# Two attention layers on one core: where a phase issues side products, divisors, loads and normalizations

## The chip, the cores and the metric

The kernel runs on one core of a Trainium2 chip. The metric is the device time of one execution in microseconds; the median of several executions is compared. A core has five engines with a queue each: TensorE (PE, its weight loads shown as PEld), VectorE (DVE), ScalarE (ACT), GpSimd (POOL) and SyncE (SP). Here SP issues most of the DMAs, POOL a few small ones.

## What is computed

Two layers on x of shape (4, 256, 64, 64), all in float32; each is a group norm (32 groups), an attention and a residual:

```python
# layer A (0): 4096 queries against 1024 keys, 8 heads of 32
q = einsum('oc,bchw->bohw', Wq, x)                 # x here is _gn(x)
k = conv2x2_stride2(x, Wk);  v = conv2x2_stride2(x, Wv)
attn = softmax((q.k + q.(rel_h + rel_w)) * 32**-0.5)
x = x_in + attn.v
# layer B (1): 4 areas of 1024 tokens, 8 heads of 32
qkv = conv1x1(x, w_qkv) + b_qkv                    # x here is _gn(x)
out = softmax(q.k * 32**-0.5).v                    # within an area
out = out + depthwise_conv7x7(v_full, w_pe) + b_pe
x = x_in + conv1x1(out, w_proj) + b_proj
```

## The kernel before, in words

**Units, steps, phases.** A block is one layer of one batch element: A0 to A3, then B0 to B3. A block has 16 units: 8 chunks of 512 queries, twice 4 heads each; 128 units in all. A unit has 8 steps, one for each 128 keys. A step is four score products (keys on the partitions, 512 queries each), exp on ACT, the product of p with v accumulated in one PSUM bank `av`, and an addition of p into `acc` on DVE, from which the softmax's divisors come. A *phase* works on one and a half steps: three PSUM pairs of scores, so three exponentials of 128x1024 (two at line 334, `exp_full`, the third, of two half steps, at line 345, `exp_half`). There are 683 phases.

**A phase in the order of issue** (the main loop at the end of `direct_path`): `scores(f)` issues the score products (line 296) on PE. Then the exponentials `exps[0]`, `exps[1]`, `exps[2]` on ACT. Between them stand `add_ready`, which issues the additions of the phase before (line 369, DVE), and, where a unit ends within the phase, the last weighted products of the old unit (`accumulate`, line 359) and `evict`, the copy of `av` to SBUF as `av_sb` (line 961, ACT, two buffers). Then come the planned actions (`do`), the divisors or side parts, the weighted products of the phase before, perhaps more side parts, and another `evict`. The scheduling is manual: every engine gets its instructions in the order in which the code issues them, apart from a merge of the engines' streams.

**The score banks.** The three pairs change roles from phase to phase: the first half product of the next phase needs the pair that the second exponential has read, the first full product that of the first, the second full product that of the third.

**Side work.** All other products on PE go as *tasks* through the deque `side` and one PSUM bank (`ps_side`, tag `side`, one buffer): k0ps, v0ps, q0ps (layer A's k, v, q), k1ps, q1ps, vals_ps (layer B's k, q, v), conv_ps (the depthwise convolution as matrix products) and ops (the projection). A task is a generator of 2 or 4 *parts*; `advance` runs one. Its last part also issues the copy out of the bank, on ACT, or for ops an addition into `xm` on DVE (line 682). `need` runs tasks early where a consumer is already due. `task` appends; `soon_tasks` puts tasks behind the first one.

**The plan.** `at(g, j, f)` puts an action at step j of unit g; `do` runs all actions of the steps that a phase covers: loads (SP's DMAs), normalizations on ACT (`normalize`, line 261, in place on hq, hv, h, or into taps), additions, statistics, and the tasks' entry into `side`. `plan_norm` makes the group statistics: `aggregate` (DVE, line 230), `means` (a product gm on PE, line 235, a copy and three small DVE operations), two steps later `variances` (a product gv, line 243, and three POOL operations).

**Divisors.** When all of a unit's additions have been issued, the unit is in `to_divide`. `divisors` sums acc over the partitions by products with ones (line 378, into the side bank `den`), and `divide` copies it to `den_sb` (line 395, ACT) and sends four rows by DRAM into `few` (lines 396 and 397, POOL). At step (g+2, 0) `reciprocals` (lines 403 to 407) inverts `few` on DVE and broadcasts it by DRAM into `rb` (one buffer). At (g+2, 4) `multiply` (line 410, DVE) makes `att` from `av_sb` and `rb`. Behind it come layer A's `add_residual` and `store_chunk` (lines 534 to 540), or layer B's `add_conv` (line 667) and `project`.

Of the kernel before, what the change touches and what calls it, by code (L numbers as in the profile page):

```python
# [24 lines left out]
NKT = MK // P  # L25
# [34 lines left out]
def direct_path(  # L60
# [125 lines left out]

    side = deque()
    now, last = [-1], len(BLOCKS) * UNITS * NKT  # L190

    def task(parts, f, *args):
        side.append([parts, f(*args)])

    def soon_tasks(tasks):

        for n, (parts, f, *args) in enumerate(tasks):
            side.insert(1 + n, [parts, f(*args)])

    def advance():  # L200
        side[0][0] -= 1
        next(side[0][1], None)
        if side[0][0] == 0:
            side.popleft()

    def need(made, key):
        while key not in made:
            advance()
        return made[key]


    stats, norms = {}, {}

# [5 lines left out]
    def plan_norm(key, g, j):  # L219

        name = f"{key[0]}{key[1]}"
        made = {}

        def aggregate():
            for tag, cols in (("mv", 2), ("gmean", 1), ("dev", 1), ("gvar", 1)):
                shape = [P, CT, cols] if cols > 1 else [P, CT]
                made[tag] = pool.tile(shape, FP, tag=tag, name=f"{tag}_{name}", bufs=2)
            mv = made["mv"]
            for t in range(CT):
                V.bn_aggr(out=mv[:, t, :], in_=stats[key][:, t].rearrange("p c s -> p (c s)"))  # L230

        def means():
            mv, mean, dev = made["mv"], made["gmean"], made["dev"]
            ps = ps_side(f"gm_{name}")[:, :CT]
            T.matmul(ps, lhsT=gmat, rhs=mv[:, :, 0], start=True, stop=True)
            S.copy(mean, ps)
            V.tensor_sub(dev, mv[:, :, 0], mean)
            V.tensor_mul(dev, dev, dev)
            V.tensor_add(dev, dev, mv[:, :, 1])

        def variances():
            ps = ps_side(f"gv_{name}")[:, :CT]
            T.matmul(ps, lhsT=gmat, rhs=made["dev"], start=True, stop=True)
            S.activation(made["gvar"], ps, AF.Identity, bias=eps)
            norm = pool.tile([P, 2, CT], FP, tag="norm", name=f"norm_{name}", bufs=8)
            shift, rstd = norm[:, 0, :], norm[:, 1, :]
            G.tensor_tensor(rstd, made["gvar"], neghalf, ALU.pow)
            G.tensor_tensor(shift, made["gmean"], rstd, ALU.mult)
            G.tensor_scalar(shift, shift, -1.0, None, ALU.mult)
            norms[key] = shift, rstd  # L250

        at(g, j, aggregate)
        at(g, j + 1, means)
        at(g, j + 3, variances)

    def normalize(key, dst, src, t, by_vector=False):
        shift, rstd = norms[key]
        if by_vector:
            V.tensor_scalar(dst, src, rstd[:, t : t + 1], shift[:, t : t + 1], ALU.mult, ALU.add)
            return  # L260
        S.activation(dst, src, AF.Identity, bias=shift[:, t : t + 1], scale=rstd[:, t : t + 1])  # L261
# [121 lines left out]
    def divide(g, unit):  # L383

        if g == len(units) - 1:

            rb = pool.tile([P, CH], FP, tag="p", name="rb", bufs=PB)
            V.reciprocal(rb, dens[g])  # L388
            V.tensor_mul(unit[4]()[:, unit[0], :], avs.pop(g), rb)  # L389
            spare.extend((dens.pop(g), rb))  # L390
            return
        den_sb = pool.tile([P, CH], FP, tag="den", name="den_sb", bufs=1)
        few = pool.tile([P, 2, CH // HD], FP, tag="few", name="few", bufs=2)
        rows = dram.tile([4, CH], FP, tag="rows", name=f"rows_{g}", bufs=4)
        S.copy(den_sb, dens.pop(g))  # L395
        G.dma_start(rows, den_sb[0:P:HD, :])  # L396
        G.dma_start(few[:, 0, :], rows.rearrange("h (q n) -> (h q) n", n=CH // HD))  # L397
        made = {}

        def reciprocals():  # L400
            rb = made["rb"] = pool.tile([P, CH], FP, tag="rb", name="rb", bufs=1)
            recs = dram.tile([4, CH], FP, tag="recs", name=f"recs_{g}", bufs=4)
            V.reciprocal(few[:, 1, :], few[:, 0, :])
            V.tensor_reduce(sums[:, :, g], few, AX.X, ALU.add)  # L404
            G.dma_start(recs.rearrange("h (q n) -> (h q) n", n=CH // HD), few[:, 1, :])  # L405
            for h in range(4):
                G.dma_start(rb[HD * h : HD * h + HD, :], recs[h : h + 1, :].to_broadcast([HD, CH]))  # L407

        def multiply():
            V.tensor_mul(unit[4]()[:, unit[0], :], avs.pop(g), made["rb"])  # L410

        at(*((g + 2, 0) if g < len(units) - 2 else (g + 1, 6)), reciprocals)
        at(g + 2, 4 if g < len(units) - 2 else 0, multiply)

    def att_of(key):
        if key not in atts:
# [4 lines left out]
    def plan_a(b, u, prep):  # L421
# [108 lines left out]
        def load_residual(c):  # L530
            xcs[c] = load_chunk(b, c, "xc")
# [10 lines left out]
        for c in range(NCH):  # L542
            g = u + 2 * c
            at(g - 3, 4, lambda c=c: fetch(c))
            for t in range(CT):
                at(g - 2, 1 + 2 * t, lambda c=c, t=t: norm_chunk(c, t))
            for qd in range(2):
                at(g - 2, 4, lambda c=c, qd=qd: task(2, make_q, c, qd))
            at(g + 2, 4, lambda c=c: load_residual(c))
            at(g + 3, 5, lambda c=c: add_residual(c))  # L550
            at(g + 3, 6, lambda c=c: store_chunk(c))
        return [
            (
                n % 2,
# [9 lines left out]
    def plan_b(b, u):  # L564
# [148 lines left out]
                    V.tensor_scalar(bad, count, -1.0, float(P), ALU.mult, ALU.add)  # L713

        for c in range(NCH):
            g, j = u + 2 * c + 3, 5
            if b == B - 1 and c == NCH - 1:
                for t in range(CT):
                    at(g - 2, 2 + t, lambda c=c, t=t: load_rest(c, t))
                at(g - 2, 4, lambda c=c: load_residual(c))  # L720
                at(g - 1, 1, lambda c=c: add_conv(c, [0]))
                at(g - 1, 3, lambda c=c: project_last(c))
                continue
            for t in range(CT):
                at(g - 1, 3 + 4 * t, lambda c=c, t=t: load_rest(c, t))
            at(g, 2, lambda c=c: load_residual(c))
            at(g, j, lambda c=c: add_conv(c))
            at(g, j + 2, lambda c=c: soon_tasks([(2, project, c, to) for to in range(CT)]))
        return [
# [186 lines left out]
    for i, (layer, b) in enumerate(BLOCKS):  # L916
        u = i * UNITS
        if layer == "A":
            units += plan_a(b, u, u - UNITS)
            plan_norm(("B", b), u + UNITS + 1, 7)  # L920
        else:
            units += plan_b(b, u)
    plan_zeros(2)
    for b in range(B):
        for c in range(NCH):
            plan_values(b, c, (17.8, 42, 54.5, 67)[b] + (2.0, 1.5, 1.3, 2.2)[b] * c)
        for n in range(C // 16):
            plan_conv(b, n, (36, 58, 75.5, 93.5)[b] + (1.36, 1.06, 1.1, 1.1)[b] * n)

# [47 lines left out]
    def side_parts(budget):  # L977

        mine, done = side[0] if side else None, 0
        while done < budget and side and side[0] is mine:  # L980
            advance()
            done += 1

    f = step = 0
    before = []
    while f < PHASES or before or plan or side or to_add or to_divide:
        now[0] = step
        exps = scores(f) if f < PHASES else [lambda: None] * 3
        exps[0]()
        due = bool(to_divide)  # L990
        add_ready()
        due = bool(to_divide) if f >= PHASES else due
        cut = next((n for n in range(1, len(before)) if before[n][0] // NKT != before[0][0] // NKT), 0)
        for s, u in before[:cut]:
            accumulate(s, u)
        exps[1]()
        if cut:
            evict(before[0][0] // NKT)
        exps[2]()
        while step < -(-3 * (f + 1) // 2):  # L1000
            do(*divmod(step, NKT))
            step += 1
        waiting = sum(n for n, _ in side)
        whole = side[0][0] if side else 0
        if due:
            g = to_divide.popleft()
            divisors(g, *([last - 1] if g == final else []))
            if g < final:
                divide(g, units[g])
        else:  # L1010
            side_parts(2)
        for s, u in before[cut:]:
            accumulate(s, u)
        add_ready()
        if due:
            side_parts(4)
        elif whole > 2 or waiting > 7:
            side_parts(2)
        if before:
            evict(before[-1][0] // NKT)  # L1020
        before = []
        if f < PHASES:
            full, half = parts_of(f)
# [600 lines left out]
```

## Time and profile before

| what | us |
|---|---|
| median of 3 runs (3458.95 to 3462.72) | 3460.3 |
| the profiled execution, device time | 3467.67 |
| its span | 3465.9 |
| PE busy with matmuls / with weight loads | 3186.5 / 1394.4 |
| DVE busy (of it additions, line 369) | 2526.4 (2123.7) |
| ACT busy (of it exponentials, lines 334 and 345) | 2468.6 (2036.5) |
| POOL busy | 486.1 |
| granted TensorE clock, mean | 0.977 |

ACT's 2036.5 is 1162.2 + 619.6 into p and 167.2 + 87.5 into acc. Busy time is the union of an engine's instructions; matmuls overlap each other and their ends are modelled. A row of waits gives the engine and line that waited, the engine and line whose end released it, and the total, the number and the longest of these waits. A mean over the span hides that phases differ: they hold no side part, or up to five.

### The profile page before, as it was taken

How to read it: one execution, taken by the hardware profiler on the slowest of the kernel's cores; microseconds unless marked ns; L12 is line 12 of the kernel's file. 1: busy time of each engine (PE TensorE's matmuls, PEld its weight loads, DVE VectorE, ACT ScalarE, POOL GpSimd, SP SyncE). 2: the span in 40 equal slices, each digit the busy share in tenths (PEclk: the TensorE clock that was granted, in tenths of full speed). 3: DMA queues.
4: the chain of work that ended last, by engine and by line, in shares of the span. 5: the costliest groups of instructions: out<-in, count | busy, mean ns of one | idle time of the engine just before them, and what ended most of it. 6: DMA issues, size and time to landing. Idle time of an engine off the chain costs nothing. (4 is left out here: it accounts for less than half of the span.)

```text
span 3465.9 us, 87567 instructions
## 1 busy us (share of the span) xinstructions
PE 3186.5 (92%) x36218; PEld 1394.4 (40%) x36218; DVE 2526.4 (73%) x2719; ACT 2468.6 (71%) x2988; POOL 486.1 (14%) x923
## 2 busy tenths in 40 slices
PE   7999898999989998888999999999999999999997
PEld 4444333443334443333434344444334444433332
DVE  3677786667867767676677677777678777788887
ACT  3777676776767777676777677777667777777775
POOL 0111111111111111111111111111111111111111
PEclk9999999999999999999999999999999999999998
DMA  4232333354544456556766675765555555422222
GB/s 169 54 82 72 82 95 78 85 114 99 124 98 119 127 128 157 126 133 145 182 174 168 146 174 137 180 177 146 142 131 138 147 151 141 130 63 77 77 51 54
DMA packets 648233, 422.26 MB, mean 122 GB/s; under 512 B 411772, under 2 KB 556636, under 8 KB 647832
## 3 DMA queue, kind: packets, MB, share of 16 engines
q1 hardware_dynamic: 619384, 380.11, 43.2%
q0 software_dynamic: 28448, 36.48, 4.5%
q8 instruction: 292, 4.78, 0.6%
q14 instruction: 109, 0.89, 0.1%
HBM read 318.32 MB, written 98.09 MB: 120 GB/s over the span
## 5 line engine op out<-in xcount | busy, mean ns | idle before, releaser
L369 DVE TENSOR_TENSOR acc<-acc,p 128x1024 f32<-128x1024 f32 x1790 | 2123.7, 1220 | 716.7 <-PE av L359 322.5
L334 ACT ACTIVATE p<-s 128x1024 f32<-128x1024 f32 x1194 | 1162.2, 1026 | 479.8 <-PE s L296 445.0
L345 ACT ACTIVATE p<-s 128x1024 f32<-128x1024 f32 x598 | 619.6, 1036 | 8.2 <-DVE acc L369 4.3
L296 PE MATMUL s<-q,k_A 32*128 32x256 f32 (+1 forms) x5464 | 591.7, 520 | 22.4 <-ACT p L334 17.9
L296 PE MATMUL s<-q,k_B 32*128 32x256 f32 (+1 forms) x5456 | 569.8, 513 | 12.5 <-ACT p L334 11.7
L359 PE MATMUL av<-p,v_A 128*32 128x256 f32 (+1 forms) x4784 | 473.6, 503 | 0.0
L296 PEld LDWEIGHTS s<-q,k_A 32*128 32x128 f32 x5464 | 327.3, 186 | 332.8 <-issue 89.1
L296 PEld LDWEIGHTS s<-q,k_B 32*128 32x128 f32 x5456 | 332.8, 184 | 312.6 <-issue 87.5
L359 PE MATMUL av<-p,v_B 128*32 128x512 f32 (+1 forms) x4776 | 453.6, 490 | 0.0
L407 POOL DMA_DIRECT2D rb<-recs x508 | 252.0, 501 | 448.7 <-DMA recs<-few 373.5
L405 POOL DMA_DIRECT2D recs<-few x127 | 69.7, 549 | 1571.4 <-DVE sums L404 1302.4
L359 PEld LDWEIGHTS av<-p,v_A 128*32 128x32 f32 x4784 | 146.7, 112 | 264.4 <-issue 234.6
L359 PEld LDWEIGHTS av<-p,v_B 128*32 128x32 f32 x4776 | 145.3, 110 | 262.2 <-issue 236.8
L334 ACT ACTIVATE acc<-s 128x1024 f32<-128x1024 f32 x172 | 167.2, 1025 | 109.3 <-PE s L296 109.3
L378 PE MATMUL den<-acc,ones 128*32 128x512 f32 x1024 | 150.0, 627 | 25.9 <-DVE acc L369 12.9
L164 PE MATMUL ops<-cv,wp_sb 128*32 128x512 f32 x1024 | 132.9, 637 | 37.3 <-DVE cv L667 25.6
L164 PE MATMUL q0ps<-hq,wq_sb 128*32 128x512 f32 x1024 | 127.8, 611 | 31.4 <-ACT hq L261 22.2
L164 PE MATMUL vals_ps<-hv,wqkv_sb 128*32 128x512 f32 x1024 | 127.1, 611 | 30.6 <-ACT hv L261 19.0
L164 PE MATMUL k1ps<-h,wqkv_sb 128*32 128x512 f32 x1024 | 122.8, 597 | 10.3 <-ACT den_sb L395 10.3
L397 POOL DMA_DIRECT2D few<-rows x127 | 71.2, 561 | 434.1 <-DMA rows<-den_sb 426.0
L164 PE MATMUL k0ps<-taps,wkv 128*32 128x256 f32 x2048 | 125.9, 394 | 5.8 <-ACT den_sb L395 2.8
L396 POOL DMA_DIRECT2D rows<-den_sb x127 | 74.6, 588 | 385.3 <-ACT den_sb L395 382.2
(99 smaller groups left out, 2179.5 us busy)
## 6 DMA issues: line engine op xcount, KB each, us to landing
rows<-vals SPq DMA_DIRECT2D x384, 195.9 KB
rb<-recs POOLq DMA_DIRECT2D x508, 64.0 KB, 3.2
share<-vals SPq DMA_DIRECT2D x128, 195.9 KB
vala<-vout SPq DMA_DIRECT2D x128, 144.0 KB
vals<-vout SPq DMA_DIRECT2D x128, 144.0 KB
vc<-vala SPq DMA_DIRECT2D x64, 288.0 KB
band<-mats SPq DMA_DIRECT2D x96, 176.0 KB
hq<-in_x SPq DMA_DIRECT2D x32, 512.0 KB
```

Source lines behind the costliest of these rows:

```text
L164: T.matmul(out[cols, :], lhsT=lhsT[:, cols], rhs=rhs, start=start, stop=stop)
L296: return T.matmul(out, lhsT=unit[2]()[rows, unit[0], j * P : (j + 1) * P], rhs=unit[1]()[rows, cols], start=True, stop=True)
L334: S.activation(p, (a, b)[n], AF.Exp, scale=SCALE)
L345: S.activation(p, c.rearrange("p b (l n) -> p b l n", l=2), AF.Exp, scale=SCALE)
L359: T.matmul(out, lhsT=v[:, j, unit[0] * P + HD * h : unit[0] * P + HD * h + HD], rhs=rhs, start=(j == 0 and not u), stop=(j == NKT - 1), sk ...
L369: V.tensor_add(to, to, p)
L378: T.matmul(dens[g][HD * h : HD * h + HD, :], lhsT=ones, rhs=p(h), start=(n == 0), stop=(n == len(sets) - 1),)
L396: G.dma_start(rows, den_sb[0:P:HD, :])
L397: G.dma_start(few[:, 0, :], rows.rearrange("h (q n) -> (h q) n", n=CH // HD))
L405: G.dma_start(recs.rearrange("h (q n) -> (h q) n", n=CH // HD), few[:, 1, :])
L407: G.dma_start(rb[HD * h : HD * h + HD, :], recs[h : h + 1, :].to_broadcast([HD, CH]))
```

## The change

It touches the order of issue alone; no product, addition or byte is added or left out.

1. A task in `side` carries a mark, set when its first part has run; `begun()` tells whether the first task is under way.
2. In a phase the second exponential is issued ahead of an ending unit's weighted products, and the third after the divisors or side parts. The actions (`do`) go to the phase's end.
3. Side parts: two per phase (one if no more than three parts wait); two more after the weighted products only where fewer than two were run, over five wait and no task is under way (always at the end, when no phase is left). Before: two, and up to four more.
4. Divisors wait until no task is under way.
5. `means` and `variances` go through a deque `quick`, one at a phase's end when no task is under way; `normalize` runs them early where it needs them.
6. `multiply` goes from (g+2, 4) to (g+3, 0). Behind it residual loads, `add_residual`, `store_chunk`, `add_conv`, its loads and the projections go four steps later too; the statistics of layer B as well, and the values of the first batch element 0.6 units.

```diff
 def task(parts, f, *args):
-        side.append([parts, f(*args)])
+        side.append([parts, f(*args), False])
...
     def advance():
         side[0][0] -= 1
+        side[0][2] = True
         next(side[0][1], None)
...
+    def begun():
+        return bool(side) and side[0][2]
+
+    def soon(f):
+
+        if now[0] < 0:
+            f()
+        else:
+            quick.append(f)
...
-        at(g, j + 1, means)
-        at(g, j + 3, variances)
+        at(g, j + 1, lambda: soon(means))
+        at(g, j + 3, lambda: soon(variances))
...
-        at(g + 2, 4 if g < len(units) - 2 else 0, multiply)
+        at(*((g + 3, 0) if g < len(units) - 3 else (g + 2, 6) if g < len(units) - 2 else (g + 2, 0)), multiply)
...
-            at(g + 2, 4, lambda c=c: load_residual(c))
-            at(g + 3, 5, lambda c=c: add_residual(c))
-            at(g + 3, 6, lambda c=c: store_chunk(c))
+            at(g + 3, 0, lambda c=c: load_residual(c))
+            at(g + 4, 1, lambda c=c: add_residual(c))
+            at(g + 4, 2, lambda c=c: store_chunk(c))
...
-            g, j = u + 2 * c + 3, 5
+            g, j = (u + 2 * c + 4, 1) if b < B - 1 or c < NCH - 2 else (u + 2 * c + 3, 7)
...
-                at(g - 1, 3 + 4 * t, lambda c=c, t=t: load_rest(c, t))
-            at(g, 2, lambda c=c: load_residual(c))
+                at(g - 2, 7 + 4 * t, lambda c=c, t=t: load_rest(c, t))
+            at(g - 1, 6, lambda c=c: load_residual(c))
...
-            plan_norm(("B", b), u + UNITS + 1, 7)
+            plan_norm(("B", b), u + UNITS + 2, 3)
...
         exps[0]()
-        due = bool(to_divide)
         add_ready()
         due = bool(to_divide) if f >= PHASES else due
+        exps[1]()
         cut = next((n for n in range(1, len(before)) if before[n][0] // NKT != before[0][0] // NKT), 0)
         for s, u in before[:cut]:
             accumulate(s, u)
-        exps[1]()
         if cut:
             evict(before[0][0] // NKT)
-        exps[2]()
-        while step < -(-3 * (f + 1) // 2):
-            do(*divmod(step, NKT))
-            step += 1
-        waiting = sum(n for n, _ in side)
-        whole = side[0][0] if side else 0
-        if due:
+        waiting = sum(n for n, *_ in side)
+        used = 0
+        if due and not begun():
+            used = 1
             g = to_divide.popleft()
             divisors(g, *([last - 1] if g == final else []))
             if g < final:
                 divide(g, units[g])
         else:
-            side_parts(2)
+            used = side_parts(2 if waiting > 3 or due else 1)
+        exps[2]()
         for s, u in before[cut:]:
             accumulate(s, u)
         add_ready()
-        if due:
-            side_parts(4)
-        elif whole > 2 or waiting > 7:
+        if not begun() and used < 2 and waiting > 5 or f >= PHASES:
             side_parts(2)
         if before:
             evict(before[-1][0] // NKT)
+        if quick and not begun():
+            quick.popleft()()
+        while step < -(-3 * (f + 1) // 2):
+            do(*divmod(step, NKT))
+            step += 1
```

More of the change, by code (lines that the diff above doesn't have):

```diff
@@ L185, in at @@
         plan.setdefault((g, j), []).append(f)
-    side = deque()
+    side, quick = deque(), deque()
     now, last = [-1], len(BLOCKS) * UNITS * NKT
     def task(parts, f, *args):
-        side.append([parts, f(*args)])
+        side.append([parts, f(*args), False])
     def soon_tasks(tasks):
         for n, (parts, f, *args) in enumerate(tasks):
-            side.insert(1 + n, [parts, f(*args)])
+            side.insert((1 if side and side[0][2] else 0) + n, [parts, f(*args), False])
     def advance():
         side[0][0] -= 1
+        side[0][2] = True
         next(side[0][1], None)
@@ L252, in plan_norm @@
         at(g, j, aggregate)
-        at(g, j + 1, means)
-        at(g, j + 3, variances)
+        at(g, j + 1, lambda: soon(means))
+        at(g, j + 3, lambda: soon(variances))
     def normalize(key, dst, src, t, by_vector=False):
+        while key not in norms:
+            while begun():
+                advance()
+            quick.popleft()()
         shift, rstd = norms[key]
@@ L925, in direct_path @@
         for c in range(NCH):
-            plan_values(b, c, (17.8, 42, 54.5, 67)[b] + (2.0, 1.5, 1.3, 2.2)[b] * c)
+            plan_values(b, c, (18.4, 42, 54.5, 67)[b] + (2.0, 1.5, 1.3, 2.2)[b] * c)
         for n in range(C // 16):
@@ L982, in side_parts @@
             done += 1
+        return done
     f = step = 0
     before = []
-    while f < PHASES or before or plan or side or to_add or to_divide:
+    while f < PHASES or before or plan or side or quick or to_add or to_divide:
         now[0] = step
         exps = scores(f) if f < PHASES else [lambda: None] * 3
+        due = bool(to_divide)
         exps[0]()
-        due = bool(to_divide)
         add_ready()
         due = bool(to_divide) if f >= PHASES else due
+        exps[1]()
         cut = next((n for n in range(1, len(before)) if before[n][0] // NKT != before[0][0] // NKT), 0)
@@ L1020, in direct_path @@
             evict(before[-1][0] // NKT)
+        if quick and not begun():
+            quick.popleft()()
+        while step < -(-3 * (f + 1) // 2):
+            do(*divmod(step, NKT))
+            step += 1
         before = []
```

## The prediction

> **What bounds the kernel now.** I read the busy shares first, then who PE waits for, then who DVE waits for, then single phases on the time line, with the windows' granted clock beside them.
>
> ```profile
> PE 3186.5 (92%) x36218; PEld 1394.4 (40%) x36218; DVE 2526.4 (73%) x2719; ACT 2468.6 (71%) x2988; POOL 486.1 (14%) x923
> ```
>
> PE is the bound, but a busy PE here isn't a PE at its peak. So I cut the trace at the first score weight load (L296) of each phase. From 82.94 to 3432.42 us there are 682 phases, 3349 us. Typical ones, as windows (us from:to, length, busy time of PE, PEld, DVE, ACT, POOL, clock, DMA):
>
> ```profile
> 2426.50:2429.68 3.18, 3.01 (x36) 1.44 (x32) 3.15 (x4) 1.99 (x3) 0.00 (x0) 1.00 0.76 202
> 1833.69:1838.35 4.66, 4.66 (x52) 1.96 (x48) 4.59 (x7) 3.43 (x4) 0.55 (x1) 1.00 0.61 169
> 1843.01:1849.44 6.43, 5.73 (x60) 2.12 (x56) 3.29 (x3) 3.78 (x5) 2.31 (x5) 1.00 1.04 154
> 2441.84:2456.79 14.95, 7.95 (x48) 2.06 (x48) 11.15 (x11) 5.06 (x5) 0.56 (x1) 0.66 0.43 121
> ```
>
> The first has no side part, the second two, the third divisors and two parts, the fourth two parts and a stall. Undisturbed phases with one part are 3.80 long, with two 4.66, with four 6.40: a part is 0.853 and a phase without any would be 2.95. It is 3.18, because the first half product needs the bank of the second exponential: too little work for PE, so ACT sets its length. Nominal length of all: 682 x 2.95 + 1075 parts x 0.853 = 2932; so some 415 us are lost. PE's waits tell where (us, times, longest):
>
> ```profile
> PE av L359 <- ACT av_sb L961: 47.5, 42, 1.5
> PE ops L164 <- DVE cv L667: 25.6, 8, 7.0
> PE q0ps L164 <- ACT hq L261: 22.2, 10, 2.3
> PE vals_ps L164 <- ACT hv L261: 19.0, 5, 6.3
> PE conv_ps L890 <- ACT den_sb L395: 12.1, 14, 2.1
> PE gm_B L235 <- DVE mv_B L230: 11.2, 3, 4.7
> ```
>
> and behind the long ones stands DVE, which waits for the broadcast reciprocals in front of `multiply`:
>
> ```profile
> DVE att_A L410 <- DMA rb<-recs: 70.7, 21, 9.6
> DVE att_B L410 <- DMA rb<-recs: 32.2, 10, 7.0
> ```
>
> The fourth window shows the whole chain on the time line (start, duration, engine, line; in brackets the idle time before it and what ended it):
>
> ```profile
> 2445.50 0.69 DVE L410 TENSOR_TENSOR att_B<-av_sb,rb 128x512 f32<-128x512 f32 x1 [7.03 <-DMA rb<-recs]
> 2446.11 3.68 DVE L369 TENSOR_TENSOR acc<-acc,p 128x1024 f32<-128x1024 f32 x3
> 2447.42 2.16 ACT L334 ACTIVATE p<-s 128x1024 f32<-128x1024 f32 x2 [3.59 <-DVE acc L369]
> 2449.71 2.10 DVE L667 SCALAR_TENSOR_TENSOR cv<-cv,bpe_sb,att_B 128x512 f32<-128x512 f32 x2
> 2450.89 3.64 PE L164 MATMUL ops<-cv,wp_sb 128*32 128x512 f32 x16 [7.00 <-DVE cv L667]
> ```
>
> DVE stands 7.03 us at `multiply`; the additions come late, so the exponentials find no free p; `add_conv` comes late, so PE stands 7.00 at the projection, and then runs at half clock (0.66 in the window). This phase loses 14.95 - 4.66 = 10.3 us. 29 phases lose over 3 us each, 164 in all; in 39 phases the granted clock is under 1, always in whole stretches of 3.4, 6.8 or 10.2 us at one half, begun in or just after such a stall. The clock is thus no cause of its own: it goes with the stalls.
>
> [...]
>
> So the 415 us are: 156 phases without side part and eviction at 0.81 (0.22 of their own, and 0.59 in the next one, whose second full score product waits for the late third exponential) = 126; waits for av_sb 47.5; waits of the seven side products for den_sb, 45.8 by the same list; the rest, 196, are stalls with their half clock.
>
> **The change, part by part.** Work on PE, ACT, DVE and the bytes moved stay what they are; all is order. The counts are from the order of the instructions in the two built programs.
>
> *Even side parts.* Phases with 0, 1, 2, 3, 4, 5 parts (divisors count one): before 198, 77, 296, 42, 60, 8; after 49, 233, 355, 44, 0, 0, with 1075 parts in both. Without side part and eviction there are 37 instead of 156: 37 x 0.81 = 30 (before 126). Evictions with too little work behind them to cover av_sb: 38 instead of 42 waits, shorter ones, since in 26 of them a part stands between (before in none): 31 (before 47.5). Phases with four or five parts, where PE waits for the copy of one task before the next (6.40 and more), are gone.
>
> *The third exponential after the side parts.* On ACT, the copies of side products stood behind L345; now 87 + 40 den_sb and 333 others stand ahead of it. For den_sb with two parts behind (third window; den_sb at 3.92 to 4.52 in its phase, the next product at 4.57 instead of 3.65) the copy now starts at 3.01 and PE needn't wait: 45.8 goes to nearly 0. The price: the third exponential ends later. In an undisturbed phase it starts 3.01 and ends 4.04 after the phase's start; with a 0.60 copy ahead it ends at 4.55 (that is where it ends today in phases with av_sb ahead of it); behind a two-part product, which is ready 2.0 us after its first weight load at 1.52 (k1ps: 1847.59, its copy 1849.58), at 5.05 to 5.15. The next phase's second full product takes it without loss until 0.27 after that phase's start, and is late by all that comes after (in the trace its weight load follows the exponential's end by 0.05). With lengths 3.80 and 4.66: one part and den_sb, 4.55 - 3.80 - 0.27 = 0.44 to 0.48, x 87 = 38; one part with another copy 0.45 x 70 = 32; two parts 0.12 x 220 = 27; two parts, copy and av_sb 0.79 x 39 = 31; three parts nothing. Sum 128. Bounds: 0, if the score products' other half covers it, and 230, if every copy ahead costs 0.5; I take 128, by the rows with av_sb ahead.
>
> [...]
>
> *Multiplications later* (from 4 steps after the reciprocals to 8; by phases 2 to 4 before, 4 to 6 after, so some 22 us instead of 9 to 17). Waits so far reached 9.6 us beyond that: the 102.9 us of DVE waits go. What is late next: `few` for the reciprocals (2 phases after the divisors in 10 units instead of 3; only 5.2 us of waits today), cheap. The residual loads, `add_residual`, `store_chunk`, `add_conv`, the conv loads and the projections move by the same 4 steps with the same distances; on SP's queue they now stand behind the side stores of their phase. Side products come 2 to 3.5 phases later in the mean; the tightest, a q of layer B, is still done 2 phases ahead of its scores (7 before), k 7 (13), the last convolution 22 (25). None is forced early by a consumer.
>
> *Loads, normalizations, statistics at the phase's end.* A task can no longer start in the phase that issues its normalization: 22.2 + 19.0 of waits go with their half clock, and with `soon` the gm_B and gvar waits (11.2 and 6.9). ACT has the normalizations (0.83 to 1.25 us) behind a later third exponential: some 200 phases, of which those with the 1.25 form delay the next first exponential by about 0.4; I take 20, bounds 0 and 50.
>
> *What is left of the 196.* The first two phases lose 12 and little changes there; den waits for acc (12.9) depend on DVE's lag, which gets less. I take 45; bounds 10 and 196.
>
> *End.* The projections of the next to last chunk move into the tail, in front of the last reciprocal (3.35): one product and xm, about +3.
>
> **Sum:** 30 + 31 + 128 + 20 + 45 = 254 lost instead of 415: -161, +3 for the end: -158. The profiled execution took 3467.7 (span 3465.9), 7 over the median of the timed runs, 3460.3. Against that median: 3460 - 158 = 3302.
>
> **Rivals.**
> 1. *Stalls only move* (d stays). For it: it's not shown that every long stall comes from rb; some normalizations wait on late exponentials alone. Against: in the three longest an rb wait of 4.6 to 7.0 us stands just ahead. With 140 to 196 left instead of 45, the gain is 63 down to 7: 3397 to 3453.
> 2. *Slower: eviction waits for `multiply`.* av_sb has two buffers, so the eviction of unit g waits for the multiplication of g-2. It stood 3 to 4 phases and 8 to 10 additions ahead; now 1 phase and 0 to 2 additions. While ACT waits, the third exponential and the next unit's first products do too. The additions (paired with the exponentials in order) end 4.2 us after them in the median, 7.7 or more in the worst tenth, and the multiplication has about a phase and a half, some 6 us. Against it: the lag falls at a unit's end, where three exponentials have no addition. It decides from 158 / 127 = 1.25 us a unit; with 2 us: +254, 3302 + 254 = 3556.
> 3. *Copies cost nothing*, stalls all gone: 30 + 31 + 10 + 10 lost, -330: 3130; half their price, 3195.
>
> **How the numbers follow.** Forecast 0.62 (3235 to 3390: the bounds of its terms, 0 to 50 and 10 to 120, about the taken ones); rival 1 0.18 (3390 to 3455, 0.02 of it no change); rival 2 0.10 (a tenth of it no change); rival 3 0.10 (3130 to 3235, a fifth of it over 3220). The range 3220 to 3450 leaves out rival 2, most of rival 3 and the end of rival 1, 2 in 10. Within 0.2% (7 us, what a measurement can tell from no change) 0.03, slower 0.09, faster 0.88.
>
> **What would show it.** Right: DVE's waits for rb under 10 us, hq, hv and cv gone from PE's list, a mean granted clock over 0.99 (0.977 now), phases of two parts at 4.7 to 4.9, one-part phases with den_sb at 4.2 to 4.3. New on PE's list would be s <- ACT p L360 with 100 or more. Wrong: av_sb waiting for DVE att on ACT's list (rival 2), or ops, vals_ps and q0ps still with gaps over 3 us (rival 1).

## The result, and the profile after

The changed kernel takes 3250.2 us (median of four, 3247.9 to 3252.4) against 3461.5 us for the kernel before on the same chip: ratio 0.938, 95% interval 0.936 to 0.941. It is 211 us faster; 158 were forecast. The profiled execution took 3248.9 us (span 3246.8).

The busy times first (engine, busy us, share of the span, instructions):

```profile
PE 3130.2 (96%) x36218; PEld 1357.5 (42%) x36218; DVE 2526.9 (78%) x2719; ACT 2485.4 (77%) x2988; POOL 489.6 (15%) x923
```

Instructions and work are the same; PE's own busy time fell by 56 us, which goes with fewer stretches at half clock (mean granted clock 0.995 instead of 0.977). Who PE waits for now (us, times, longest):

```profile
PE av L374 <- ACT av_sb L976: 30.8, 44, 2.3
PE s L311 <- ACT p L360: 21.9, 17, 10.6
...
PE s L311 <- ACT p L349: 10.7, 22, 1.3
PE ops L164 <- DVE cv L682: 4.4, 1, 4.4
...
PE k0ps L164 <- ACT den_sb L410: 2.9, 1, 2.9
```

(The lines stand 15 further down in the code: L349 is the full exponential, L360 the third, L384 the addition, L410 the copy to den_sb, L425 `multiply`.) The normalized inputs hq and hv are gone, cv is left once, in the tail, den_sb for the seven side products nearly gone. DVE's list, of which three lines answer to the question asked before:

```profile
DVE vout L824 <- DMA vals<-vout: 20.0, 2, 12.9
DVE few L418 <- DMA few<-rows: 19.8, 7, 5.2
...
DVE att_B L425 <- DMA rb<-recs: 0.5, 1, 0.5
```

The 102.9 us for rb are 0.5. A new wait stands at the head: two of 20.0 us in all for the store of vals to leave a buffer.

Cut into phases as before, the 682 phases take 3131.1 us instead of 3349.5. Against 2.96 us a phase and 0.853 a part, 198.3 us are lost instead of 416.7. By the phases' number of side parts, with those that lose over 3 us each kept apart (number: us lost):

| kernel | over 3 us each | no part | one | two | three | four, five | sum |
|---|---|---|---|---|---|---|---|
| before | 29: 163.6 | 194: 120.9 | 71: 6.5 | 284: 50.4 | 40: 47.0 | 63: 28.3 | 416.7 |
| after | 4: 31.0 | 48: 34.4 | 233: 71.6 | 355: 40.8 | 41: 20.4 | 0 | 198.3 |

The numbers add up to 681, because the first two phases are counted as one, against one nominal length. That pair stands in the first column, with 5.8 us before and 3.7 after, of which 2.96 are no loss. So 133 us came from the long stalls, 86 from phases without a part; two, three and more parts give 64, and phases with one part take 65 back. 39 phases had a granted clock under 1; now it is 4.

Windows of after show the price that was taken for the third exponential behind the copies (us from:to, length, busy time of PE, PEld, DVE, ACT, POOL, clock, DMA). They are two parts with a copy, undisturbed; one part of divisors, and the phase after it; divisors and two parts, with an eviction; a long one:

```profile
1680.75:1685.45 4.70, 4.70 (x52) 1.87 (x48) 4.19 (x4) 3.54 (x5) 0.52 (x1) 1.00 0.72 147
1646.66:1650.47 3.81, 3.81 (x45) 1.71 (x41) 3.51 (x3) 3.81 (x6) 1.40 (x3) 1.00 0.73 191
1650.47:1655.51 5.04, 5.04 (x52) 1.66 (x48) 4.26 (x5) 3.88 (x5) 1.16 (x3) 1.00 0.88 259
1767.21:1772.79 5.58, 5.58 (x61) 2.04 (x57) 2.31 (x5) 4.28 (x6) 1.03 (x2) 1.00 0.69 84
1999.25:2014.29 15.04, 7.89 (x60) 2.17 (x56) 5.72 (x10) 5.55 (x7) 3.11 (x6) 0.77 0.53 107
```

A two-part phase is 4.70, not the 4.66 + 0.12 that was taken. Divisors and two parts take 5.58, where they took 6.43 in the prediction's third window: the copy of the divisors now stands ahead of the third exponential, and PE's next product hardly waits for it. The divisors' phase has its 3.81 as before, and the next one, with two parts, 5.04: 0.38 over 4.66. How that comes is seen on the time line of these two (start, duration, engine, line; in brackets the idle time before and what ended it):

```profile
1647.91 1.94 ACT L349 ACTIVATE p<-s 128x1024 f32<-128x1024 f32 x2
...
1649.74 0.59 ACT L410 COPY den_sb<-den 128x512 f32<-128x512 f32 x1
...
1650.20 1.05 ACT L360 ACTIVATE p<-s 128x1024 f32<-128x1024 f32 x1
1650.46 0.31 PEld L311 LDWEIGHTS s<-q,k_B 32*128 32x128 f32 x8 [0.41 <-ACT den_sb L410]
...
1651.31 0.41 PEld L311 LDWEIGHTS s<-q,k_B 32*128 32x128 f32 x8 [0.53 <-ACT p L360]
```

The copy stands between the second exponential and the third, which starts 3.54 us after its phase's start (1646.66) instead of 3.01. It ends at 1651.25, and the next phase's second full product starts at 1651.31, 0.84 us after the phase's start at 1650.47. Without delay it starts 0.32 after. It is 0.52 late, and that phase 0.38 longer, so something of the delay is hidden. Over all phases but the two that end in the long stalls below, this lateness sums to 150 us in 430 of them. How much is hidden comes out of the same cutting: in phases with one or two parts a product that is up to 0.1 us late makes the phase no longer; one that is 0.26, 0.52, 0.62 or 1.04 late makes it 0.13, 0.38, 0.47 or 0.90 longer (medians). About 0.14 us of each delay is free, and what exceeds it is paid in full.

The new long stall on the time line:

```profile
2112.88 5.01 SPq L848 DMA_DIRECT2D vals<-vout  x2
...
2123.39 0.07 DVE L824 MEMSET vout<- 128x16 f32 x1 [12.92 <-DMA vals<-vout]
...
2123.51 0.70 ACT L835 ACTIVATE vout<-vals_ps,bqkv_sb 128x512 f32<-128x512 f32 x1 [11.14 <-DMA vals<-vout]
...
2124.11 1.01 ACT L360 ACTIVATE p<-s 128x1024 f32<-128x1024 f32 x1
...
2125.17 2.08 PE L311 MATMUL s<-q,k_B 32*128 32x512 f32 x8 [10.55 <-ACT p L360]
```

The copy of a vals product needs one of the five buffers `vc`, which it shares with the convolution's inputs; the next one to come free is emptied by the store issued at 2112.88, which lands 10.5 us later (DVE's wait ends with it). DVE, which only clears the buffer's edges, stands 12.92, ACT 11.14. The third exponential stands behind the copy and, 1.06 us after it started, PE goes on. This happens twice (phases of 15.04 and 19.36 us): 23 us of the 31.0 in the table. Here ACT took copy and exponential in their order of issue: the last score product of this exponential ends at 2110.40 on the time line, and it stood through the 11.14 us behind the copy.

Last, the rival by which it would have become slower, on ACT's list:

```profile
ACT av_sb L976 <- DVE att_A L425: 18.0, 10, 5.1
...
ACT av_sb L976 <- DVE att_B L425: 8.6, 12, 1.8
```

The eviction waits for `multiply` in 22 of 128 units, 26.6 us of ACT's time; that is 0.2 us a unit, and the point from which it decided was 1.25.

### The profile page after: what moved, and what is told of

Same layout as the page of the kernel before. It is cut to its first block, busy times and chain, and to the rows that moved or that the text cites. A ratio compares the mean times of both kernels' runs of the same rounds, so it can differ in the third digit from the quotient of the medians.

```text
span 3246.8 us, 87669 instructions
## 1 busy us (share of the span) xinstructions
PE 3130.2 (96%) x36218; PEld 1357.5 (42%) x36218; DVE 2526.9 (78%) x2719; ACT 2485.4 (77%) x2988; POOL 489.6 (15%) x923
## 4 chain that ended last, share of the span: by engine, by line
PE 75%; ACT 7%; DVE 6%; issue 5%; DMA 5%; SPq 1%; POOL 0%; ACTq 0%; DVEq 0%; POOLq 0%
PE s L311 26%; PE av L374 20%; DVE acc L384 5%; PE k1ps L164 3%; PE ops L164 3%; PE den L393 3%; PE conv_ps L905 3%; PE q1ps L164 3%; PE v0ps L164 3%; PE k0ps L164 3%; ACT p L349 3%; PE vals_ps L164 3%; PE q0ps L164 2%; ACT p L360 1%; DMA rows<-vals 1%
## 5 line engine op out<-in xcount | busy, mean ns | idle before, releaser
L384 DVE TENSOR_TENSOR acc<-acc,p 128x1024 f32<-128x1024 f32 x1790 | 2118.4, 1220 | 580.7 <-PE av L374 303.7
L349 ACT ACTIVATE p<-s 128x1024 f32<-128x1024 f32 x1194 | 1163.3, 1024 | 394.3 <-PE s L311 380.4
L360 ACT ACTIVATE p<-s 128x1024 f32<-128x1024 f32 x598 | 619.0, 1035 | 0.0
L311 PE MATMUL s<-q,k_B 32*128 32x256 f32 (+1 forms) x5456 | 590.7, 517 | 23.7 <-ACT p L360 18.6
L311 PEld LDWEIGHTS s<-q,k_B 32*128 32x128 f32 x5456 | 312.8, 183 | 349.1 <-ACT p L360 95.9
L311 PEld LDWEIGHTS s<-q,k_A 32*128 32x128 f32 x5464 | 314.7, 183 | 329.4 <-ACT p L360 70.6
L374 PE MATMUL av<-p,v_A 128*32 128x256 f32 (+1 forms) x4784 | 449.9, 486 | 0.0
L349 ACT ACTIVATE acc<-s 128x1024 f32<-128x1024 f32 x172 | 166.9, 1023 | 65.5 <-PE s L311 65.2
L393 PE MATMUL den<-acc,ones 128*32 128x512 f32 x1024 | 141.2, 611 | 2.2 <-DVE acc L384 2.1
L164 PE MATMUL ops<-cv,wp_sb 128*32 128x512 f32 x1024 | 125.5, 605 | 6.9 <-DVE cv L682 4.4
L164 PE MATMUL q1ps<-h,wqkv_sb 128*32 128x512 f32 x1024 | 123.9, 596 | 0.0
```

The costliest lines, as they stand in the source:

```text
L164: T.matmul(out[cols, :], lhsT=lhsT[:, cols], rhs=rhs, start=start, stop=stop)
L311: return T.matmul(out, lhsT=unit[2]()[rows, unit[0], j * P : (j + 1) * P], rhs=unit[1]()[rows, cols], start=True, stop=True)
L349: S.activation(p, (a, b)[n], AF.Exp, scale=SCALE)
L360: S.activation(p, c.rearrange("p b (l n) -> p b l n", l=2), AF.Exp, scale=SCALE)
L374: T.matmul(out, lhsT=v[:, j, unit[0] * P + HD * h : unit[0] * P + HD * h + HD], rhs=rhs, start=(j == 0 and not u), stop=(j == NKT - 1), sk ...
L384: V.tensor_add(to, to, p)
```

## The experiments

All times are medians, ratios are against the kernel before of the same chip session, with the 95% interval. Items are those of the list of the change.

**1. The third exponential ahead again, alone.** One line of the changed kernel moves:

```diff
+        exps[2]()
         waiting = sum(n for n, *_ in side)
 ...
             used = side_parts(2 if waiting > 3 or due else 1)
-        exps[2]()
```

> The changed kernel with one thing undone: the third exponential stands ahead of the divisors and side parts again, all else as changed. Theory (the copies ahead of the third exponential have the price that the prediction gave them, about 128 us, and save den_sb waits of about 0.92 us in the 40 phases with divisors and two more parts, 37 us): the time falls by 128 - 37 = 91 us, from 3250 to about 3160, and PE waits for den_sb come back with 30 to 45 us. Rival (the late third exponential is hidden by the other half of the score products, and an early copy frees the side bank): no gain, or slower, 3250 to 3290.

3229.2 us (0.932, 0.930 to 0.934): 21 us less than the changed kernel, far from the 90 that the theory had. The waits for den_sb came back as expected; the two largest of the rows of PE's list, of 32.5 us in all:

```profile
PE q1ps L164 <- ACT den_sb L410: 12.0, 16, 1.0
PE k0ps L164 <- ACT den_sb L410: 5.4, 4, 3.6
```

**2. Ahead, but behind the divisors' copy where side products follow.**

```diff
+        late = due and not begun() and waiting > 5
+        if not late:
+            exps[2]()
 ...
-        exps[2]()
+        if late:
+            exps[2]()
```

> As the run before, but in phases where divisors are followed by side parts the third exponential stays behind the copy of the divisors. Theory: the whole price of the copies is saved and no den_sb wait comes back: 3250 - 128 = about 3122, some 35 us under the run before. Rival (copies cost nothing): 3250, and no difference from the run before beyond 10 us.

3201.1 us (0.924, 0.922 to 0.926): 49 less than the changed kernel, 28 less than in experiment 1. So the place behind the copy is right for the divisors that are followed by side products (worth 28 us), and costs 49 for the other copies. The lateness of the second full products fell from 150 to 36.5 us, as the mechanism has it; but 114 us of lateness cost 49 us of time. The forecast had priced it 1 for 1 beyond a margin, which was too small. What exceeds the free 0.14 us sums to 97 us in the changed kernel and 25 here, 72 less. Set against the changed kernel phase by phase (the long ones left out, and differences of over 0.1 us counted), 147 phases are shorter by 65 us in all, and 32 are longer, by 17: in the one at 2443.24, PE waits 0.80 us for the copy of k_B, which now stands behind the third exponential.

**3. Multiplications back, alone.** All that item 6 moves goes back to where it was, `multiply` to (g+2, 4) and so on.

> The changed kernel with the multiplication, and all that follows it, back at four steps after the reciprocals. Theory (the waits of DVE for rb are the root of the long stalls and their half clock): DVE waits about 100 us for rb again, and the time rises by 60 to 120 us, to 3310 to 3370, with a mean clock of 0.985 or less. Rival (with even side parts and tasks that start a phase after their normalization such waits are absorbed): within 25 us of 3250, clock above 0.99.

3262.6 us (0.942, 0.940 to 0.944), 12 more than the changed kernel; DVE's waits:

```profile
DVE att_A L425 <- DMA rb<-recs: 76.3, 23, 12.1
...
DVE att_B L425 <- DMA rb<-recs: 37.4, 18, 5.8
```

113.7 us of waits are back, more than before the change, and they cost little. The 12 hides that the two stalls at vout are not in this run (the row is gone; by the shift, not by design), 23 us; by that the waits cost some 35 (an estimate). My theory fell here: the waits for rb were not what most of the lost time hung on.

**4. The old budget for parts and divisors back, alone.**

```diff
-        if due and not begun():
+        if due:
 ...
-            used = side_parts(2 if waiting > 3 or due else 1)
+            used = side_parts(2)
 ...
-        if not begun() and used < 2 and waiting > 5 or f >= PHASES:
+        if due:
+            side_parts(4)
+        elif whole > 2 or waiting > 7:
             side_parts(2)
```

> The changed kernel with the old rule for the number of side parts in a phase, and divisors that don't wait for a task's end (186 phases without side part and eviction instead of 37, and phases with four and five parts). Theory (each such phase costs 0.81 us, 120 us more, and 20 us more of waits for av_sb, less some 20 us of copies ahead of the third exponential): 3250 + 120 = about 3370. Rival (only the rb waits mattered, even parts are worth little because DVE or ACT sets the pace anyway): under 3285.

3348.0 us (0.967, 0.965 to 0.969): 98 more. It has 220 phases without a part, which lose 129.2 (48 and 34.4 in the changed kernel), and PE's wait for the eviction is up again:

```profile
PE av L374 <- ACT av_sb L976: 49.2, 43, 3.9
```

Only 7 phases lose over 3 us (36.1): with late multiplications and the end-of-phase actions in place, bursts alone don't bring the long stalls back.

**5. Multiplications later, on the kernel before.** The reverse of experiment 3, in the kernel before.

> The kernel before, with the later multiplication (and what follows it) alone. The run with the multiplication put back in the changed kernel lost only 12 us. Theory A (rb waits and normalizations in the tasks' own phase make the long stalls together, and either part alone takes most of them away): 3461 falls by 70 to 130 us, to 3330 to 3390, and DVE's waits for rb go. Theory B (the long stalls come from tasks that start in the phase of their normalization; rb waits matter little anywhere): falls by less than 40 us, to 3425 to 3465, though the rb waits go.

3434.9 us (0.993, 0.991 to 0.996), 27 less. DVE's waits for rb are gone (0.6 us); long stalls are 21 phases with 94.0 instead of 29 with 163.6. The time is in the range of theory B, but the stalls answer as in theory A: 70 us went out of them, and about 40 came back, most of it here: 222 phases without a part lose 134.7 (194: 120.9), those with three 68.2 (47.0); PE's wait for av_sb, part of these, is 56.9 (47.5). PE still waits for hq, 18.9 us (22.2).

**6 and 7. The actions back in the middle of the phase (on top of 1), and then the multiplications back as well.** In 6 the `while step` loop stands right behind `exps[2]()`; 7 adds the edits of 3.

> The run with the third exponential ahead of the side parts (3229 us), with loads, normalizations and the tasks' entry also back at their old place behind that exponential and ahead of the side parts. Theory A: without rb waits this costs little, 0 to 30 us: 3229 to 3260. Theory B: hq and hv waits on PE come back with 20 us or more, and with half clock 40 to 100 us: 3270 to 3330.

> As the run before, with the multiplication back as well: of the change only the even side parts, the waiting divisors and the group statistics one by one are left. Theory A: now the long stalls are back, 80 to 150 us more than the run before: 3320 to 3390, clock 0.985 or less. Theory B: no more than the run before plus 35. If both are small, the even parts themselves took the stalls away, and it stays under 3290.

6: 3254.4 us (0.941, 0.939 to 0.944), 25 more than experiment 1, as in its theory A. 7: 3292.0 us (0.952, 0.949 to 0.954), 38 more than 6, not the 80 and above of theory A. What is left of the change in 7 is the parts' even budget, the waiting divisors, the statistics one by one and the second exponential ahead, and it keeps most of the gain, though DVE waits for rb as much as ever (first fence) and PE hardly for what hangs on it (second):

```profile
DVE att_A L425 <- DMA rb<-recs: 76.8, 18, 9.9
...
DVE att_B L425 <- DMA rb<-recs: 30.9, 14, 6.9
```

```profile
PE ops L164 <- DVE cv L682: 11.5, 6, 4.4
...
PE vals_ps L164 <- ACT hv L276: 6.9, 2, 4.6
PE q0ps L164 <- ACT hq L276: 6.3, 3, 2.2
```

**8. Values of the last batch element apart (on top of 2)**, so that the store of one pair of chunks has left before the next needs its buffer:

```diff
-            plan_values(b, c, (18.4, 42, 54.5, 67)[b] + (2.0, 1.5, 1.3, 2.2)[b] * c)
+            plan_values(b, c, (18.4, 42, 54.5)[b] + (2.0, 1.5, 1.3)[b] * c if b < 3 else 67 + 4 * (c // 2) + 1.2 * (c % 2))
```

> The run with the third exponential mostly ahead of the side parts (3201 us), and the value projections of the last batch element moved in between the v loads of layer B, so that vout finds a free vc buffer without waiting for the store of vals. Theory (the two stalls at units 78 and 82 are a wait for vc's five buffers): the wait of DVE vout for vals goes from 23.9 us to under 3, and the time falls by 15 to 25 us, to 3176 to 3186. Rival (the stores are late by themselves): the wait moves to other units, 3195 to 3205.

3204.8 us (0.927, 0.925 to 0.929): no better than 2. The wait moved and grew, as in the rival (23.9 in 2); DVE has

```profile
DVE vout L824 <- DMA vals<-vout: 38.0, 3, 16.4
```

**9 and 10. A sixth buffer** for `vc` and vout (`bufs=6`; cout and tap give one of their two for the space), in the changed kernel, and in that of experiment 2.

> The changed kernel with six buffers of vc instead of five (and one of the convolution's output instead of two, for the room). Theory (the two new stalls are a wait of vout for a free buffer, and through the copy ahead of the third exponential for PE): DVE's wait of vout for the store of vals goes under 3 us, both long phases go, and 3250 falls by 18 to 26 us to 3224 to 3232. Rival (the stores are late, and the next buffer waits as the last one did): less than 6 us.

> The same two buffer numbers with the third exponential mostly ahead of the side parts (3201 us). Theory: both gains add, 3201 - 20 = 3175 to 3185. Rival: 3195 to 3205.

9: 3228.7 us (0.933, 0.930 to 0.936), 22 less than the changed kernel, as its theory had it. DVE's wait at vout is gone, and the stretch that was one long phase is full work:

```profile
1999.25:2014.29 15.04, 15.04 (x158) 6.09 (x160) 13.31 (x15) 11.29 (x14) 3.12 (x6) 1.00 0.79 173
```

10: 3182.7 us (0.919, 0.916 to 0.922; 3176 to 3195): the best of all, as its theory had it; 68 under the changed kernel and 279 under the one before.

**11. Only the statistics one by one, on the kernel before** (item 5, with item 1's mark and the second exponential ahead, and with a line of the change that its list leaves out: `soon_tasks` puts its tasks ahead of a first task that is not under way). This is 7 without the even budget and the waiting divisors.

> The kernel before with the marks of tasks and the group statistics one by one at a phase's end, and nothing else of the change: its phases have the same numbers of parts as before. The run with even parts on top of this had 3292 us. Theory A (even parts took that gain): 3425 to 3461, at most 35 us of gain, since only the waits of gm and behind gvar go. Theory B (the group statistics are what the even parts seemed to bring): under 3400.

3451.0 us (0.996, 0.995 to 0.997), in the range of theory A. So the step from here to 7, the even budget with the waiting divisors, is worth 159 us. PE's waits in 11, to be held against the second fence of 7:

```profile
PE ops L164 <- DVE cv L682: 28.7, 8, 7.2
...
PE q0ps L164 <- ACT hq L276: 24.5, 11, 2.3
PE vals_ps L164 <- ACT hv L276: 17.1, 5, 5.9
```

## Why the prediction came out as it did

The runs make a chain from the kernel before to the changed one, one part at a time, with the table from above for each:

| step | us | gain | over 3 us each | no part | sum lost |
|---|---|---|---|---|---|
| before | 3461.5 | | 29: 163.6 | 194: 120.9 | 416.7 |
| statistics one by one (11) | 3451.0 | 11 | 26: 141.7 | 194: 121.4 | 402.8 |
| even parts, waiting divisors (7) | 3292.0 | 159 | 17: 72.0 | 45: 31.6 | 238.5 |
| multiplications later (6) | 3254.4 | 38 | 9: 45.8 | 51: 34.2 | 204.5 |
| actions at the phase's end (1) | 3229.2 | 25 | 4: 29.6 | 48: 33.1 | 180.2 |
| third exponential behind (after) | 3250.2 | -21 | 4: 31.0 | 48: 34.4 | 198.3 |

(11, 7 and 6, and 1 come from three sessions in which the kernel before took 3465, 3457 and 3463; by the ratios the steps are 13, 155, 36, 31 and -22.) The direction held, and 3250 lies in the range; of 254 us forecast to stay lost, 198 stayed. That the sum came so near is in part luck: the gain in the stalls was given to the wrong steps, and the part that was given too little went in with the same change. By the prediction's steps:

- **Even side parts: right, and worth more than forecast.** The forecast gave them 112 us (126 to 30, and 47.5 to 31). Taken back alone they cost 98 (experiment 4); put on top of 11 they bring 159, 70 of it out of the long stalls, in which the forecast gave them no share. Waits for av_sb are 30.8. That phases without a part lose 120.9 and 34.4 looks like the 126 and 30, but these are not the same phases: the forecast has those without an eviction, at 0.81 each. Before, the 42 with an eviction lose 66 of the 120.9, the others 55 of their own; and the phase behind, whose second full product is 0.59 late, is 0.45 longer (median) and not 0.59.
- **"Multiplications later ... the 102.9 us of DVE waits go": they went, but they were not the root that they were taken for.** The 151 us that were to go out of the 196 hung on this step and on the actions at the phase's end. Measured, the waits' removal is worth 38 (7 to 6), some 35 (experiment 3 with the vout stalls set apart) and 27 (experiment 5), the actions' move 25. In the long stalls the later multiplications and the even parts overlap: they lose 163.6 before, 141.7 with the statistics alone (11), 94.0 with late multiplications alone (5), 72.0 with even parts (7, DVE's waits for rb at 107.7 where 11 has 111.8), 45.8 with both (6). Either one takes some 70 us out of them when it comes first, but the later multiplications give about 40 back in other phases, and the even parts don't. A chain seen in one phase was taken for the cause of all. Why the even parts do it is argued: the wait of DVE seems to cost PE time where a task stands at the head of `side` whose input has just been ordered. By the order of the instructions the first q0ps product came in the phase of its normalization or the next in 31 of 32 cases before, in 14 of 32 in experiment 7, in 4 after; vals in 18 before, 7 in experiment 7, 3 after. PE's waits for hq, hv and cv, 66.8 us before, are 24.7 in 7. That a bit of backlog in `side` is what hides the lateness was not varied by itself.
- **Third exponential behind the copies, +128: right in kind, mis-sized.** It measured 49 (2 against after), and the den_sb waits it removes 28 (45.8 in the list before, 32.5 in experiment 1). Moved as a whole it is a loss of 21, not the 82 of 128 - 46. What was off is the margin in "without loss until 0.27": about 0.14 us more of each delay is free. The late product delays its own phase by 0.38 where it is 0.52 late, and phases of two parts with a copy, some 220, lose 0.05 and not 0.12. And some 17 us come back in other phases; in the one at 2443.24 because a copy that comes earlier spares PE a wait of 0.80 us for it.
- **Normalizations behind the third exponential, +20: not measured apart.** The step that moves them, with all other planned actions, gained 25 as a whole.
- **"What is left of the 196": 45 taken, 31.0 measured**, but 23 of it is the new stall at vout, which no rival had. Without it the old long stalls are nearly all gone: experiment 9 has one such phase, with 5.4 us, beside the first two counted as one.
- **What would show it:** rb under 10 (0.5), hq and hv gone (cv but once, in the tail), clock over 0.99 (0.995) and two-part phases of 4.7 were right. A den phase at 4.2 to 4.3 was wrong: the loss falls into the next phase. s <- ACT p L360 with 100 or more was wrong (21.9, of which 17.7 are the two stalls at vout): most of the lateness is not idle time of PE and isn't on its list.
- **Rivals:** 1 (stalls only move) fell. 2 (eviction waits for `multiply`) is there, at 0.2 us a unit instead of 1.25. 3 (copies cost nothing) was nearer on this term than the 128: they cost 49, two fifths of it.

About 57 us of the 198 stay unexplained (an estimate, as these terms may overlap): 31 in long phases, 49 for the copies, 31 for av_sb and some 30 in empty phases leave that much, in small losses spread over phases with one to three parts. The even budget without the waiting divisors, or alone on the kernel before, was not tried.

## What to carry to other kernels

Before a long wait is given a price, undo it alone: here the end of DVE's waits was worth 27 to 38 us, while evening out the filler work was worth 98 to 159. Spread filler evenly; a little of it queued between an input's producer and its consumer seems to hide a late input, though no run shows this alone. Where an engine takes its queue in the order of issue, as ACT did in the stall at 2112.88 (11.14 us), put what frees a buffer for the bound engine ahead of any copy that waits, unless that copy itself is waited for, and count the buffers behind that copy.

## What the runs showed of the hardware

The score products overlap each other: in the changed kernel 5456 of 517 ns each (mean, layer B) take 590.7 us together. One that started late was partly hidden: about 0.14 us of each delay was free (0.52 us late cost 0.38, 1.04 cost 0.90).

The half clock doesn't follow from the length of the gap alone. In the changed kernel gaps of 3.20 and 3.23 us between weight loads, which end at 838.16 and 786.73, came without it. In the kernel before, one of 2.43 us, which ends at 554.68, had a half-clock stretch behind it, and one of 1.92 us, which ends at 1869.97, had one from 1869.42 on. In each of these two traces the half-clock stretches after the first 50 us begin on one grid of 3.413 us, to within 0.01: in the changed kernel at 1164.58, 2004.26 and 2116.90, which are 246 and 33 steps apart. Cut on these grids, the two traces from the first phase to the last give 1847 windows at full clock. All 25 in which PE was busy for 1.40 us or less were followed by half clock, none of the 1796 with over 2.07 us, and 6 of the 26 between. The gap of 3.23 falls into two windows, which keep 2.12 and 2.39 us of work (first two lines; the third number from the end is the clock); the one of 2.43 falls into one, which keeps 1.07, and the next is at half clock (last two):

```profile
782.29:785.70 3.41, 2.12 (x20) 0.39 (x12) 3.41 (x5) 0.95 (x2) 0.00 (x0) 1.00 0.61 151
785.70:789.12 3.42, 2.39 (x24) 0.88 (x24) 2.92 (x5) 3.03 (x5) 0.55 (x1) 1.00 0.87 241
...
551.88:555.29 3.41, 1.07 (x14) 0.58 (x14) 0.00 (x0) 2.75 (x4) 0.57 (x1) 1.00 0.02 7
555.29:558.70 3.41, 3.41 (x28) 0.77 (x16) 0.87 (x1) 0.59 (x1) 1.21 (x4) 0.50 0.01 2
```

So in these traces the half clock goes with little work in a window of the grid, which needn't be idle throughout: the gap of 1.92 us lies in one with 1.66 us of work. What tells the 6 of the 26 from the others is open.

The store of vals took 10.5 us from issue to the end of DVE's wait in both of the stalls, with 5.04 and 5.01 us of it on SP's queue for two DMAs, where the next pair, just after the stalls, takes 1.97 and 1.34 us.
